# An attention and feed-forward block on one core: q's weights packed earlier, the second rows normalised in two parts, two value projections ahead of the scores, value slots by VectorE

## The chip, the core and the metric

The kernel runs on one core of a Trainium2 chip. A core has a matrix engine (TensorE, PE in the profile; its weight loads are shown apart as PEld), a vector engine (VectorE, DVE), a scalar engine for activations (ScalarE, ACT), a general engine (GpSimd, POOL) and a queue engine (SyncE, SP), and 16 DMA engines that move data. Each engine works through its own instructions in order. DMAs are issued by SP, ACT or POOL, and the issue itself takes time on that engine. The metric is the time of one execution on the device in microseconds, less is better; it is compared by the median of several runs.

## The reference

Four sequences of 1024 tokens with 256 channels go through an attention layer with 16 heads of 16 channels and then through a gated feed-forward part. Cut to what matters:

```python
x = x + _layernorm(attn(_layernorm(x), Wqkv, Wout))
x = x + _layernorm(ffn(_layernorm(x), w1, w2, h1, h2, w3))

# attn
qkv = (x @ Wqkv.T).reshape(B, S, 3, H, Dh)
scores = einsum('bhqd,bhkd->bhqk', q, k) / sqrt(Dh)
exp_x = exp(clip(scores - max(scores), -50, 50))
out = (exp_x / (sum(exp_x) + 1e-6)) @ v
return out @ Wout.T

# ffn
h = silu((x @ w1.T) * w1_s) * ((x @ w2.T) * w2_s)
h = gelu((h @ h1.T) * h1_s)
h = gelu((h @ h2.T) * h2_s)
return (h @ w3.T) * w3_s
```

## The kernel before

All tensors are in float32; products that need more than one pass are split into a high and a low part (`hi` and `lo`, type float32r). A batch is one of the four sequences; `h` counts its two halves of 512 rows (NH = 2), and a half has four row tiles of 128 (TPQ = 4).

**The opening (L1309 to L1341).** It prepares batch 0 before the loop over score tiles starts. Its parts are small steps, made by `prologue` (L329):

- `norm[h]`: statistics of the rows of a half on DVE (L97, L98), then the reciprocal root on POOL (L107).
- the first two steps of `xt[h]` (called `normalise[h]` at L1324): each applies mean and root to two of the four row tiles on DVE (L126, output `xn`).
- the last two steps of `xt[h]`: for each of two chunks of 128 channels, four transposes on PE (L363, into `pt`) and one copy of 128x512 into `xT`, which `to_scalar` (L324) does on ACT in the opening.
- `qk[0][h]`: two projections, of k (w = 1) and q (w = 0), 16 PE instructions each (L321). ACT then writes the high part (L324) and DVE the low part (L394). With the argument `(0, 1)` both chunks are done at once.
- `v`: four steps, each projecting the values of two row tiles (L321, into `pv`) and copying them to `cv`. In the opening the copy is ACT's, since `first_copy` looks at `alone` (L1314); after `alone = False` it is DVE's (L327).

`wqk_sb`, the weights of the projections, arrives padded to slots of 32 and is packed by `compact(w)` (L208), one ACT copy for k (w = 1) and one for q (w = 0).

**Stacks.** Scores are one product over a stack of 64 partitions, in which the high and low parts lie beside each other. `copies(g, w, c0, c1)` (L473) gives the 16 DMAs that fill the stack of one half of k or q for head group g; in the opening they are dealt over the queues in the order ACT, POOL, SP, POOL, SP, POOL, SP, POOL (L1319), so that each set of 16 takes two issues of ACT, eight of POOL and six of SP. Later stacks go by SP alone (L496).

**Value slots.** The weighing of values reads `vaug`, in which every head has 32 columns: 16 values and a one. `slots(b, g, t0, t1)` (L508) copies them there from `cv`, by POOL.

**The loop (L1357).** A tile is the scores of one block of 128 keys and two of the group's four heads with 512 queries: two products (L534, `s`), then one exponential on ACT (L535, `e`). A head group has 32 tiles, a batch four groups. Each turn of the loop makes up to three tiles, weighs earlier ones (L542, `acc`), folds maxima on DVE (L554, `top`), and then lets `side.take` run a few side steps: at most one with PE work in a turn. The side steps are chains, in the order in which they were added at L1344 to L1347: the rest of the values, the value slots, the projections for the upper channels (`qk[1]`), the next batch's preparation, stacks and later loads on SP, and the rounding of the feed-forward weights on POOL.

Buffers that matter: `pt`, the projections' outputs, `pv` in the opening and the scores share three PSUM buffers (`ps`); after the opening side steps use another single one (`misc`). `xn` has one buffer.

The order within an engine is the order of the program text: the scheduler of the language is off (L164).

Of the kernel before, what the change touches and what calls it, by code (L numbers as in the profile page):

```python
# [37 lines left out]
NQ = 512  # L38
# [91 lines left out]
def tile_fast(ctx: ExitStack, tc: tile.TileContext, x, wqk, wv, wo, w1, w1s, w2, w2s, h1, h1s, h2, h2s, w3, w3s, out, bad):  # L130
    nc = tc.nc
# [4 lines left out]
    NT = S // P  # L136
    NH = S // NQ
# [58 lines left out]
    with ExitStack() as actx, ExitStack() as rctx:  # L196
# [11 lines left out]
        def compact(w):  # L208
            nc.scalar.copy(wqk_sb[:, :, w], padded[:, :, w, :, 0:DH])  # L209
# [263 lines left out]
        def copies(g, w, c0=0, c1=S):  # L473

            m, i = g // GPT, g % 2

            def copy(u, j, n):
                def run(queue):
                    k = "hi" if (j // 2 == 0 if w == 0 else j % 2 == 0) else "lo"
                    r = (g % GPT) * HPG * DH + (2 * u + n) * DH  # L480
                    o = n * ROWS + j * DH
                    queue.dma_start(out=stacks[w, i, u][o : o + DH, c0:c1].bitcast(F32), in_=cq[w, m, k][r : r + DH, c0:c1].bitcast(F32))  # L482

                return run

            return [copy(u, j, n) for u in range(2) for j in range(PARTS) for n in range(2)]
# [18 lines left out]
            steps[0].ready = lambda: g < GPT or later["qk1"] == b  # L505
            return steps + [Step(done, 0, False)]

        def slots(b, g, t0=0, t1=NT):  # L508


            def run():
                nc.gpsimd.tensor_copy(  # L512
                    vaug[g % 2][:, t0:t1, :, 0:DH], cv[:, t0:t1, HPG * DH * g : HPG * DH * (g + 1)].rearrange("p t (h e) -> p t h e", e=DH)
                )
                slotted[g % 2] = b, g, t1

            return run
# [224 lines left out]
        side = Side()  # L742
        accs, tops, ends, later = {}, {}, {}, {"qk1": None}

        def add_flags(steps):

            if later.setdefault("flags", [[]])[0]:
                later["flags"][0].extend(steps)
            else:
                later["flags"] = side.add(steps)  # L750

        def begin(b):

            if b + 1 < B:
                norm, xt, qk, v, flags = prologue(b + 1, misc, to_vector)

                def first_made():
                    later["qk"] = b + 1
                    add_flags(flags[0])

                def second_made():
                    later["qk1"] = b + 1
                    add_flags(flags[1])


                steps = norm[0] + norm[1] + xt[0]
                for i, step in enumerate(qk[0][0]):
                    steps += [step, xt[1][i]]
                steps += xt[1][TPQ // 2 :] + qk[0][1]


                for m in range(DC):
                    qk[m][0][0].ready = lambda m=m: not any(at == b and g // GPT == m for at, g in outstanding)
                xt[0][TPQ // 2].ready = lambda: later["qk1"] == later["v"] == b
                v = v + [Step(lambda: later.update(v=b + 1), 0, False)]
                qk1 = sum(qk[1], [])
                for step in qk1:
                    step.gap = 2
                qk1 = qk1 + [Step(second_made, 0, False)]
                later["rest"] = [Step(lambda: side.add([Step(lambda: None, 5, False)] + qk1), 0, False)] + v  # L780

                later["chain"] = side.add([Step(lambda: None, 0 if b else 4, False)] + steps + [Step(first_made, 0, False)])

        def unit_end(b, g, h):
# [539 lines left out]
        normalise = [steps[: TPQ // 2] for steps in xt]  # L1324
        for step in norm[0] + normalise[0] + norm[1]:
            step.run()
        for h in range(NH):
            for step in xt[h][TPQ // 2 :]:
                step.run()
            for w, step in zip((1, 0), qk[0][h]):  # L1330
                if (h, w) == (0, 0):
                    compact(0)
                step.run(0, 1)
                for i, copy in enumerate(copies(0, w, h * NQ, (h + 1) * NQ)):
                    copy(queues[i % len(queues)])
                if w and h + 1 < NH:
                    for step in normalise[h + 1]:
                        step.run()
        stacked[0] = 0, 0
        v[0].run()  # L1340
        alone = False  # L1341
        load_x(1)
        early = [v[1], Step(slots(0, 0, 0, NT // 2), 0, False)]
        side.add(early + v[2:] + [Step(slots(0, 0), 0, False), Step(slots(0, 1), 0, False)] + sum(qk[1], []) + [Step(lambda: later.update(qk1=0, v=0), 0, False), Step(lambda: add_flags(flags[0] + flags[1]), 0, False)])  # L1344
# [12 lines left out]
        while weighed < len(tiles):  # L1357
# [14 lines left out]
            while halves and weighed + 2 <= n:  # L1372
                b, g, h, c, _ = tiles[weighed]
# [264 lines left out]
```

## Time and profile before

The median of three runs is 1232.06 us (1228.26 to 1233.94). The profiled execution took 1232.08 us, of which 1230.2 us lie between its first and last instruction.

| engine | busy us | share of the span | instructions |
|---|---|---|---|
| PE | 1169.1 | 95% | 7994 |
| PEld | 710.1 | 58% | 7994 |
| DVE | 841.5 | 68% | 1500 |
| ACT | 885.1 | 72% | 1049 |
| POOL | 209.1 | 17% | 279 |

The chain of work that ended last is made of PE for 58% of the span, of DVE and ACT for 12% each, of SP's queue for 6% and of DMA for 6%. Attention ends near 595 us; up to there the exponentials are busy for 483.1 us with 512 instructions of 1043 ns each, and the feed-forward part behind it is PE's, with four groups of 448 products of some 395 ns each.

In the rows shown below, a time is counted from the first instruction of the profile; a row stands for a run of like instructions, with its start, its busy time, engine, line, operation, output and inputs, and count. What stands in brackets is how long the engine was idle before it, and what ended that. "SPq" and "ACTq" are issues of DMAs on these engines. The granted clock is 1.00 at full speed.

### The profile page before, as it was taken

What the parts mean: (1) busy time and instruction counts of PE and PEld (TensorE: products, weight loads), DVE (VectorE), ACT (ScalarE), POOL (GpSimd) and SP (SyncE); (2) the same over time, 40 slices, a digit from 0 to 9 for tenths busy, and PEclk for the clock granted to TensorE, in tenths of its full rate; (3) what the DMA queues carried; (4) which work ended last, traced back from release to release, by engine and by line L of the source; (5) the groups of instructions that cost most, each with busy time, mean ns of one, the idle gap of its engine ahead of it and who ended that gap; (6) DMA issues with size and microseconds to landing.
All of it is one profiled execution on the core that took longest, in us unless ns stands there. A gap on an engine that the chain in (4) does not pass through costs nothing.

```text
span 1230.2 us, 21266 instructions
## 1 busy us (share of the span) xinstructions
PE 1169.1 (95%) x7994; PEld 710.1 (58%) x7994; DVE 841.5 (68%) x1500; ACT 885.1 (72%) x1049; POOL 209.1 (17%) x279
## 2 busy tenths in 40 slices
PE   7999999999999999999999999999999999999993
PEld 2333333333333333333578888887888878888783
DVE  3485668777687756868685756867578676784755
ACT  3798899878988989999457565576656766566651
POOL 6222035434354432000000000000000000000000
PEclk8999999999999999999999999999999999999997
DMA  4676755756666666453314341344512545125401
GB/s 132 175 183 152 172 148 134 186 135 175 152 162 154 173 168 148 96 140 128 104 34 138 119 156 52 103 171 147 178 59 97 175 156 176 62 82 199 155 7 37
DMA packets 78672, 163.66 MB, mean 133 GB/s; under 512 B 14688, under 2 KB 40928, under 8 KB 78560
## 3 DMA queue, kind: packets, MB, share of 16 engines
q1 hardware_dynamic: 68624, 131.27, 38.7%
q0 software_dynamic: 9408, 30.42, 7.7%
q8 instruction: 65, 1.06, 0.4%
q10 hardware_dynamic: 528, 0.52, 0.2%
q14 instruction: 47, 0.39, 0.1%
HBM read 98.71 MB, written 29.88 MB: 105 GB/s over the span
## 4 chain that ended last, share of the span: by engine, by line
PE 58%; DVE 12%; ACT 12%; SPq 6%; DMA 6%; issue 5%; ACTq 0%; POOL 0%; POOLq 0%; DVEq 0%
PE ph L1034 27%; PE acc L542 9%; PE pg L955 8%; ACT e L535 6%; PE s L534 6%; SPq L482 5%; PE p L321 3%; DVE lo L929 2%; ACT hi L925 2%; PE py L321 2%; DVE top L554 1%; DMA sq<-cq1lo 1%; DMA folded<-top_d 1%; PE pz L1139 1%; DVE w L1045 1%
## 5 line engine op out<-in xcount | busy, mean ns | idle before, releaser
L535 ACT ACTIVATE e<-s 128x1024 f32<-128x1024 f32 x512 | 483.1, 1043 | 53.8 <-PE s L534 44.1
L542 PE MATMUL acc<-e,vaug 128*32 128x512 f32 (+1 forms) x2424 | 258.7, 539 | 2.9 <-POOL vaug L512 2.9
L534 PE MATMUL s<-sq,sk 64*128 64x512 f32 x1024 | 189.3, 446 | 25.3 <-ACT e L535 17.1
L534 PEld LDWEIGHTS s<-sq,sk 64*128 64x128 f32 x1024 | 87.6, 185 | 172.0 <-ACT e L535 142.1
L1034 PE MATMUL ph<-hi,sq 128*128 128x512 f32 x448 | 178.1, 398 | 0.8 <-DVE w L1045 0.8
L1034 PE MATMUL ph<-lo,sq 128*128 128x512 f32 x448 | 176.7, 394 | 0.0
L1034 PE MATMUL ph<-hi,sk 128*128 128x512 f32 x448 | 176.7, 394 | 0.0
L1034 PE MATMUL ph<-lo,sk 128*128 128x512 f32 x448 | 176.4, 394 | 0.0
L107 POOL TENSOR_TENSOR rstd<-ve,minus_half 128x4 f32<-128x4 f32 (+1 forms) x34 | 38.2, 1123 | 740.6 <-DVE ve L105 681.8
L554 DVE TENSOR_TENSOR top<-top,e 128x512 f32<-128x512 f32 x192 | 138.9, 723 | 24.3 <-ACT e L535 18.5
L542 PEld LDWEIGHTS acc<-e,vaug 128*32 128x32 f32 x2424 | 61.8, 109 | 120.5 <-issue 107.8
L929 DVE TENSOR_TENSOR lo<-c,hi 128x1024 fp32r<-128x1024 f32 x48 | 58.4, 1223 | 66.0 <-ACT hi L925 66.0
L929 DVE TENSOR_TENSOR lo<-g,hi 128x1024 fp32r<-128x1024 f32 x48 | 58.8, 1226 | 58.0 <-ACT hi L925 57.7
L1034 PEld LDWEIGHTS ph<-hi,sq 128*128 128x128 f32 x448 | 84.2, 188 | 21.6 <-DVE w L1045 2.1
L1034 PEld LDWEIGHTS ph<-hi,sk 128*128 128x128 f32 x448 | 84.1, 188 | 20.0
L1034 PEld LDWEIGHTS ph<-lo,sk 128*128 128x128 f32 x448 | 84.1, 188 | 19.9
L1034 PEld LDWEIGHTS ph<-lo,sq 128*128 128x128 f32 x448 | 84.2, 188 | 19.1
L1022 ACT ACTIVATE c<-ph,h_scale 128x512 f32<-128x512 f32 x64 | 40.6, 685 | 50.1 <-PE ph L1034 50.1
L321 PE MATMUL p<-xT,wqk_sb 128*32 128x512 f32 x512 | 69.3, 622 | 4.7 <-ACT wqk_sb L209 2.6
L957 ACT ACTIVATE sg<-pg,w_scale 128x512 f32<-128x512 f32 x64 | 43.6, 688 | 35.7 <-PE pg L955 31.9
L1139 PE MATMUL pz<-w_sb,lo 128*128 128x256 f32 x256 | 61.6, 284 | 2.8 <-DVE lo L929 2.8
L958 DVE SCALAR_TENSOR_TENSOR g<-pg,w_scale,sg 128x512 f32<-128x512 f32 x64 | 47.7, 747 | 23.1 <-ACT sg L957 23.0
(183 smaller groups left out, 1735.1 us busy)
## 6 DMA issues: line engine op xcount, KB each, us to landing
sq<-h_f SPq DMA_DIRECT2D x56, 512.0 KB, 3.8
sk<-h_f SPq DMA_DIRECT2D x56, 512.0 KB, 4.5
w<-in_h_dram POOLq DMA_DIRECT2D x32, 256.0 KB, 5.2
h_f<-wr POOLq DMA_DIRECT2D x16, 512.0 KB, 4.3
x<-in_h_dram SPq DMA_DIRECT2D x16, 512.0 KB, 3.6
top_d<-top SPq DMA_DIRECT2D x30, 256.0 KB, 2.5
folded<-top_d SPq DMA_DIRECT2D x30, 256.0 KB, 3.2
h_f<-wr POOLq DMA_DIRECT2D x16, 384.0 KB, 3.7
```

What stands on the lines that cost most here:

```text
L321: nc.tensor.matmul(o[j : j + SLOT, :], w[:, j : j + SLOT], i, **flags)
L482: queue.dma_start(out=stacks[w, i, u][o : o + DH, c0:c1].bitcast(F32), in_=cq[w, m, k][r : r + DH, c0:c1].bitcast(F32))
L534: nc.tensor.matmul(s[:, a, :], stacks[1, g % 2, u][r, c * P : (c + 1) * P], stacks[0, g % 2, u][r, h * NQ : (h + 1) * NQ], start=True, sto ...
L535: nc.scalar.activation(pair(k)[:, u], s, AF.Exp)
L542: nc.tensor.matmul(acc[SLOT * i : SLOT * (i + 1), q0:q1], vaug[g % 2][:, c, i, :], pair(k)[:, i // 2, i % 2, q0:q1], start=c == 0 and q0 = ...
L554: nc.vector.tensor_max(top, top if c > 1 else pair(k - 2)[:, :, :, 0:P], pair(k)[:, :, :, 0:P])
L929: nc.vector.tensor_sub(self.lo[i].t, self.raw[i].t, self.hi[i].t.bitcast(F32))
L955: nc.tensor.matmul(p[:, k, :], homes[n][d][:, m * P : (m + 1) * P], half[:, d, :], start=d == j == 0, stop=d == DC - 1 and j == 1)
L957: nc.scalar.activation(sg, p[:, 0, :], AF.Silu, scale=scales["w1"][:, m : m + 1])
L958: nc.vector.scalar_tensor_tensor(x[i, h][c // 2].t[:, c % 2, :], p[:, 1, :], scales["w2"][:, m : m + 1], sg, ALU.mult, ALU.mult)
L1034: nc.tensor.matmul(p[:, j, :], w, half, start=start and c == n == 0, stop=c == HC // 2 - 1 and n == 1, skip_group_check=True,)
L1139: nc.tensor.matmul(p[:, j, :D], half[:, (t0 + j) * P : (t0 + j + 1) * P], homes["w3"][c], start=c == order[0] and n == 0, stop=c == order[ ...
```

## The change

It touches only the opening and the function `slots`.

- `compact(0)`, the packing of q's weights, is issued right after the turned first rows (`xT`) and ahead of k's high part; it was issued after k's stacks.
- The second rows' normalisation is issued in two parts of two row tiles: one ahead of k's low part, one behind it. Both stood behind it, together.
- k's DMA issues on ACT stay behind k's high part; q's two are held back until the second rows' `xT` copies have been issued.
- Two value projections run before the loop, not one; both are copied by ACT. The loop's first side step is now the third.
- The first half of group 0's value slots is copied before the loop and by DVE; the second half by DVE in the loop, where POOL copied the whole again. Group 1's slots stay with POOL.

```diff
-        def slots(b, g, t0=0, t1=NT):
+        def slots(b, g, t0=0, t1=NT, engine=nc.gpsimd):
 
 
             def run():
-                nc.gpsimd.tensor_copy(
+                engine.tensor_copy(
...
-        for h in range(NH):
+
+        def project_first(h, w):
+
+            qk[0][h][1 - w].run(0, 1)
+            runs = [(queues[i % len(queues)], copy) for i, copy in enumerate(copies(0, w, h * NQ, (h + 1) * NQ))]
+            for queue, copy in runs:
+                if queue is not nc.scalar:
+                    copy(queue)
+            return [copy for queue, copy in runs if queue is nc.scalar]
+
+        def turn_first(h):
+
             for step in xt[h][TPQ // 2 :]:
                 step.run()
-            for w, step in zip((1, 0), qk[0][h]):
-                if (h, w) == (0, 0):
-                    compact(0)
-                step.run(0, 1)
-                for i, copy in enumerate(copies(0, w, h * NQ, (h + 1) * NQ)):
-                    copy(queues[i % len(queues)])
-                if w and h + 1 < NH:
-                    for step in normalise[h + 1]:
-                        step.run()
+
+        turn_first(0)
+        compact(0)
+        normalise[1][0].run()
+        for copy in project_first(0, 1):
+            copy(nc.scalar)
+        normalise[1][1].run()
+        held = project_first(0, 0)
+        turn_first(1)
+        for copy in held:
+            copy(nc.scalar)
+        for w in (1, 0):
+            for copy in project_first(1, w):
+                copy(nc.scalar)
         stacked[0] = 0, 0
-        v[0].run()
+        for step in v[0:2]:
+            step.run()
+        slots(0, 0, 0, NT // 2, nc.vector)()
         alone = False
         load_x(1)
-        early = [v[1], Step(slots(0, 0, 0, NT // 2), 0, False)]
-        side.add(early + v[2:] + [Step(slots(0, 0), 0, False), Step(slots(0, 1), 0, False)] + sum(qk[1], []) + [...])
+        side.add(v[2:] + [Step(slots(0, 0, NT // 2, NT, nc.vector), 0, False), Step(slots(0, 1), 0, False)] + sum(qk[1], []) + [...])
         begin(0)
```

More of the change, by code (lines that the diff above doesn't have):

```diff
@@ L1326, in tile_fast @@
             step.run()
-        for h in range(NH):
+        def project_first(h, w):
[6 more added lines that the diff above has]
+        def turn_first(h):
             for step in xt[h][TPQ // 2 :]:
                 step.run()
-            for w, step in zip((1, 0), qk[0][h]):
-                if (h, w) == (0, 0):
-                    compact(0)
-                step.run(0, 1)
-                for i, copy in enumerate(copies(0, w, h * NQ, (h + 1) * NQ)):
-                    copy(queues[i % len(queues)])
-                if w and h + 1 < NH:
-                    for step in normalise[h + 1]:
-                        step.run()
+        turn_first(0)
[11 more added lines that the diff above has]
+                copy(nc.scalar)
         stacked[0] = 0, 0
-        v[0].run()
+        for step in v[0:2]:
+            step.run()
+        slots(0, 0, 0, NT // 2, nc.vector)()
         alone = False
         load_x(1)
-        early = [v[1], Step(slots(0, 0, 0, NT // 2), 0, False)]
-        side.add(early + v[2:] + [Step(slots(0, 0), 0, False), Step(slots(0, 1), 0, False)] + sum(qk[1], []) + [Step(lambda: later.update(qk1=0, v=0), 0, False), Step(lambda: add_flags(flags[0] + flags[1]), 0, False)])
+        side.add(v[2:] + [Step(slots(0, 0, NT // 2, NT, nc.vector), 0, False), Step(slots(0, 1), 0, False)] + sum(qk[1], []) + [Step(lambda: later.update(qk1=0, v=0), 0, False), Step(lambda: add_flags(flags[0] + flags[1]), 0, False)])
         begin(0)
```

## The prediction

> **What bounds the kernel now.** I read the page's 40 slices first, then the time-ordered rows of each engine over the first 75 us, because the diff touches only what is issued before the loop over score tiles and the first steps in it. The slices show TensorE (PE) at nine tenths or more everywhere but in the first and the last. So nothing of the later 1150 us is changed in its work; what can change is how long the opening takes, and whether the rest simply starts sooner. The rows of PE (start, duration, engine, line, operation, count, idle before and what ended it):
>
> ```profile
> 9.71 1.92 PE L321 MATMUL p<-xT,wqk_sb 128*32 128x512 f32 x16 [0.25 <-ACT xT L324]
> 14.27 3.62 PE L321 MATMUL p<-xT,wqk_sb 128*32 128x512 f32 x16 [2.64 <-ACT wqk_sb L209]
> 17.82 1.09 PE L363 MATMUL pt<-ident,xn 128*128 128x128 f32 x8
> 20.69 5.34 PE L321 MATMUL p<-xT,wqk_sb 128*32 128x512 f32 x32 [1.77 <-ACT xT L324]
> 25.84 1.91 PE L321 MATMUL pv<-wv_sb,xT 128*32 128x256 f32 x32
> ...
> 29.00 1.93 PE L321 MATMUL pv<-wv_sb,xT 128*32 128x256 f32 x32
> 30.87 0.97 PE L534 MATMUL s<-sq,sk 64*128 64x512 f32 x6
> 33.21 1.06 PE L542 MATMUL acc<-e,vaug 128*32 128x512 f32 x8 [1.37 <-POOL vaug L512]
> ...
> 42.51 1.50 PE L542 MATMUL acc<-e,vaug 128*32 128x256 f32 x16 [1.56 <-POOL vaug L512]
> ```
>
> Four holes are to be seen: 2.6 us before q's projection, 1.8 us before the second rows' projections, and twice a wait of the first weighings for POOL's copy into the value slots. The same 16 projection instructions take 1.92 us at 9.71 and 3.62 us at 14.27. The windows say why (busy time of PE, PEld, DVE, ACT, POOL with counts, then the granted clock, DMA share, GB/s); they are cut at the 3.41 us steps at which this trace's clock changes:
>
> ```profile
> 10.95:14.37 3.42, 0.78 (x12) 0.10 (x8) 2.05 (x6) 1.22 (x2) 2.76 (x4) 1.00 0.12 25
> 14.37:17.78 3.41, 3.41 (x16) 0.51 (x16) 0.00 (x0) 0.00 (x0) 2.47 (x6) 0.50 0.56 117
> 17.78:21.19 3.41, 1.64 (x20) 1.03 (x18) 0.69 (x1) 1.69 (x3) 2.35 (x5) 1.00 0.33 74
> 21.19:24.61 3.42, 3.42 (x24) 0.88 (x20) 0.01 (x1) 0.60 (x1) 1.48 (x4) 0.50 0.43 96
> ```
>
> A window in which PE was busy for 0.78 or 1.64 us is followed by one at half clock. ACT's rows show what filled the holes (ACTq is the issue of a DMA), and SP's what its queue does later:
>
> ```profile
> 12.33 1.23 ACTq L482 DMA_DIRECT2D sk<-ck0hi  x2
> 13.60 0.62 ACT L209 COPY wqk_sb<-e 128x512 f32<-128x512 f32 x1 [1.30 <-issue]
> ...
> 18.58 1.41 ACTq L482 DMA_DIRECT2D sq<-cq0hi  x2
> 20.04 1.09 ACT L324 ACTIVATE xT<-pt 128x512 f32<-128x512 f32 x2 [1.49 <-issue]
> ```
>
> ```profile
> 63.87 0.48 SPq L222 DMA_DIRECT2D wo_sb<-in_wo_dram  x1
> 69.47 0.38 SPq L572 DMA_DIRECT2D top_d<-top  x1
> ```
>
> **Part 1, q's weights packed early.** compact(0) goes from 13.60 to right behind the two xT copies, which end at 10.15, so it ends near 10.8. Its weights have landed: from 9.7 to 11.7 the DMA share is 0.00. ACT has nothing until 11.70, so the 0.62 us is hidden. q's projection then follows k's at 11.68 instead of 14.27 (2.59 us). The window 10.95:14.37 would then hold about 2.7 us of projections and some transposes, so no half clock should follow: 1.97 us instead of 3.66 (the chain's figures). q ends at 13.65, before 17.93. If the clock fell all the same, this gives back 1.7 us.
>
> Here the Trainium skill is weighed against the row. TensorE: Matmul & The Clock Gate (Part 1) gives half clock after an idle window of about 3.4 us, and its table of rules warns only of gaps over about 3 us. By it the holes of 2.6 and 1.8 us would leave the clock alone and only the holes could be won. The trace disagrees: over the grid of 3.41 us windows to 590 us, all five that were busy for 48% or less are followed by half clock, and none of those at 52% or more. I take the row; after the change no window of the opening should be under 70%. The skill's Part 4 speaks against me: transposes do not count as busy. Without them the hole is 13.65 to 15.2, at worst 1.6 of 3.41 us, still 54% busy, but near the edge; the grid of another execution may lie otherwise.
>
> **Part 2, the second rows in two parts.** POOL's root ends at 12.07. Two applies (1.38/4 = 0.345 us each) run to 12.8; k's low part (0.69) comes behind them, at 12.8 instead of 12.33; the other two end at 14.1. So the low part is 0.47 us later, and with it the first SP issue (13.05 to 13.5), which part 4 counts. The second transposes need the fourth row: last time the copy began 0.43 us after the fourth apply (8.63 to 9.06), so xT starts at 14.55, not 20.04. q's two DMA issues on ACT are now held until after the copies; that is the 1.41 us between cq0hi and xT. k's second projection starts at 14.55 + 0.61 + 0.04 = 15.2, not 20.69. It runs at full clock (1.97 for 3.25) to 17.2, q's to 19.1, v's first to 21.0. That step ended at 27.9: 6.9 us are won so far. The held issues, 15.7 to 17.1, fit before ACT's next work at 17.2.
>
> **Part 3, a second value projection ahead, slots by VectorE.** 1.91 us more before the first score: PE is free at 22.9. It only moves, since it stood at 29.00 between scores. Its copy out goes from DVE (0.69) to ACT (0.60), which idles then. The scores need q's stacked rows: SP's issue of those ends at 21.2 (part 4), plus 2.4 us to land, the median of sq: 23.6. The first tile uses the half that landed 2 us earlier. So two value projections and three tiles are done at about 24.7; before, they were done at 30.87: 6.2 us won.
>
> The DVE slots: no row of DVE copies 128x256 from SBUF; the nearest are the apply (0.345) and POOL's copy of that size (0.41). Between 0.2 and 0.5 I take 0.35, twice, on an engine that idles there (holes of 4.4 and 2.6 us before its rows at 36.07 and 39.36). They end near 24, before the weighing at 27. The second waits for v's last copy and holds up the next maxima by 0.35 at most. Both PE waits, 1.37 and 1.56, go: POOL had reached its copy at 32.75 only after sixteen stack issues, and its second at 41.51 rewrote all slots. From 30.87 to the fifth group's scores at 44.79 there were 13.92 us, of which 2.93 were these waits. Without them, but with one more half projection (0.86) because the side work is a step ahead, it ends at 24.7 + 11.85 = 36.5: **8.2 us**, with 0.86 us of work in hand. ACT agrees: its first exponential moves from 28.42 to 23.5, and of its 6.4 us of holes before 68 some 2.5 stay: 8.8.
>
> **Part 4, the queues.** The same 32 issues each: POOL's take 0.49 us, SP's stretches 3.95, 3.77, 4.16 and 3.70. Started at 13.5 and run through (a hole of 0.2 at 19.1 gone), SP ends its stacks at 29.0 instead of 33.27 and POOL near 28.7 instead of 32.75: SP is only 4.3 us ahead, less than PE. SP then works without a hole to 64.35: x, then the stacks of head group 1, whose last leaves at 61.21, now 56.9, and lands about 59.3. The tile that needs it was scored at 67.46, now 59.3: just in time, I charge 0.2. At 69.47 SP waited for the maxima after 5.1 us with nothing to do, so from there its queue follows the tiles again; it keeps pace if it is over 3.1 us ahead, and it is. The skill's SBUF — State Buffer (Who interferes with whom) says that a DVE operation in a 2-port mode blocks POOL's descriptor writing for its whole length; with six such operations near POOL's issues that is at most 6 x 0.35 = 2.1 us, POOL's end 30.8, still ahead. The row beside the applies now: POOL's issues took 0.70, 0.52 and 0.61 there, not 0.49: 0.36 in all. I take 0.3; nobody waits for it.
>
> **Sum.** 8.2 − 0.2 = 8.0 us. The profiled execution took 1232.08 us (span 1230.2 and 1.9 around it), and the median of the three is 1232.06, so I predict 1224.0. The later kernel repeats the same turns, each released by tiles; I charge it nothing.
>
> **Rivals.** (a) *SP sets the gain.* If its issues lengthen because they now meet in one block, or group 1 comes later than I count, PE waits at the first tile of group 1 and only SP's 4.3 us remain: 1227.8. For: SP has no hole from 25 to 64 us, and PE does wait 2.86 us for sq at 101.67. Against: the 5.1 us hole at 69. (b) *More.* The 0.86 in hand and a shorter wait at 101.67 (2.86) count fully: 8.0 + 0.9 + 1.9 = 10.8, 1221.3. (c) *Slower: the side steps, one turn earlier, meet the stack transfers.* Projections of the next batch overwrite cq while stacks are read from it; DVE already waits there in five places (14.0 us together, by the waits of DVE's low parts on sq and sk landings). A turn is 3.2 us; if each wait grows by a turn and stands on PE's path, 5 x 3.2 = 16 − 8 = 8 slower: 1240. It decides from 2.5 such turns on. Against: those steps are released only when their stacks have been issued. (d) *The clock drops once or twice anyway*: 1.7 to 3.4 us back, 1225.7 to 1227.4, joined with (a) in the range.
>
> **Numbers.** Forecast (1222.5 to 1225.5) 0.55; (a) and (d) 0.25; (b) 0.12; (c) 0.04; the gain lost in later turns, 1232, 0.04. A measurement here tells about 0.5%, 6.2 us, from no change, so under 1225.9 is faster: all of (b) and of the forecast and a little of (a), 0.68; slower 0.04; same 0.28. The range from 1219.5 to 1229.5 takes in (a), (b) and (d) with the medians' scatter.
>
> **What would show it.** Right: no half clock between 7.5 and 30 us; q's projection at 11.7 with 1.9 us; xT at 14.6; first exponential at 23 to 24.5; no PE wait on vaug; top_d of group 0 some 8 us before 69.47. Wrong: half clock at 14 or 21 us; PE waiting for sq near 59; new waits of DVE's low parts on transfers after 100 us.

## The result and the profile after

| | median us (range, runs) | ratio to before, 95% interval |
|---|---|---|
| before, in the same comparison | 1229.90 (1226.38 to 1233.94, 20) | |
| after | 1228.45 (1224.95 to 1232.57, 20) | 0.9990 [0.9978, 1.0002] |

No change can be told: the forecast of 1224.0 was 4.45 us too low, and its range, up to 1229.5, holds the time only because it reached to the rivals. About half of the miss is the starting point: the forecast began at 1232.06, a median of three, and twenty runs of before gave 1229.90. The profiled execution of after took 1230.18 us with a span of 1228.4, against 1232.08 and 1230.2.

The opening did what was forecast up to 22 us. PE's rows of after (start, duration, engine, line, operation, count, idle before and what ended it):

```profile
9.71 3.64 PE L321 MATMUL p<-xT,wqk_sb 128*32 128x512 f32 x32 [0.25 <-ACT xT L324]
...
15.16 3.64 PE L321 MATMUL p<-xT,wqk_sb 128*32 128x512 f32 x32 [0.25 <-ACT xT L324]
18.62 3.64 PE L321 MATMUL pv<-wv_sb,xT 128*32 128x256 f32 x64
22.91 0.70 PE L534 MATMUL s<-sq,sk 64*128 64x512 f32 x2 [0.66 <-DMA sq<-cq0hi]
25.02 1.07 PE L534 MATMUL s<-sq,sk 64*128 64x512 f32 x4 [1.41 <-ACT e L535]
26.02 3.47 PE L321 MATMUL pv<-wv_sb,xT 128*32 128x256 f32 x32
```

k's and q's projections are one run without a hole, the second rows start at 15.16 (20.69 before), and two value projections end at 22.3. Then PE waits twice, and the third value projection takes 3.47 us for what lasted 1.9. The windows of after (busy time of PE, PEld, DVE, ACT, POOL with counts; granted clock, DMA share, GB/s), cut at the 3.41 us steps at which this trace's clock changes, show why:

```profile
18.94:22.35 3.41, 3.32 (x64) 1.72 (x56) 0.69 (x1) 1.22 (x3) 3.08 (x8) 1.00 0.64 130
22.35:25.77 3.42, 1.45 (x6) 0.84 (x6) 0.37 (x1) 1.59 (x2) 3.42 (x8) 1.00 0.54 122
25.77:29.18 3.41, 3.41 (x34) 1.38 (x32) 0.00 (x0) 1.94 (x2) 3.15 (x7) 0.50 0.58 119
```

The two half-clock windows of before, at 14 and 21 us, are gone; a window with PE busy for 1.45 of 3.42 us is followed by a new one at 25.77. ACT's rows have the turned rows and the first exponential where they were expected (14.55; 23 to 24.5):

```profile
14.51 1.09 ACT L324 ACTIVATE xT<-pt 128x512 f32<-128x512 f32 x2 [0.31 <-PE pt L363]
...
23.65 1.02 ACT L535 ACTIVATE e<-s 128x1024 f32<-128x1024 f32 x1 [0.73 <-PE s L534]
```

SP's rows show the stack that PE waited for at 22.9 and, later, the maxima of group 0 (`top_d`, at 69.47 before). The second wait is for the same stack: its last transfer landed at 24.68, in the same moment in which the exponential ended that the bracket names.

```profile
17.34 2.03 SPq L482 DMA_DIRECT2D sq<-cq0hi  x1
...
51.70 0.53 SPq L572 DMA_DIRECT2D top_d<-top  x1
...
56.73 0.34 SPq L575 DMA_DIRECT2D folded<-top_d  x1
...
66.42 0.38 SPq L572 DMA_DIRECT2D top_d<-top  x1
```

One issue took 2.03 us where its neighbours take 0.5 to 0.8. And 66.42 instead of 69.47 is a gain of 3.05 us, not of 8.

**Where it went.** Exponentials are 512 in both kernels and in the same order, so their starts serve as a ruler. The lead of an exponential is its start in the profiled execution of before less its start in the run, in us (worked out from the rows of L535). The expectations further down count from another zero of the trace; their leads of after are 0.15 us higher.

```
exponential             0     12     33     45     48     64     80     96    112    256    511
after                4.77   4.92   4.78   4.67   2.93   2.93   2.79   3.04   0.89   1.75   2.10
e1_pack              5.00   3.60   3.60   3.59   3.59   3.59   4.66   4.65   2.68   3.49   4.13
e2_pool_slots        4.02   4.80   5.20   2.32   2.19   2.20   3.46   3.71   1.01   1.28   3.55
e3_three             2.93   6.21   5.91   3.11   2.98   2.98   1.96   2.20   2.66   2.16   4.73
e4_fill              4.49   6.52   4.92   4.41   3.92   3.92   2.34   2.57   2.95   2.64   3.46
f1_wo_pool           4.62   6.69   5.47   2.58   2.45   2.46   6.47   6.71   4.15   3.81   6.46
f2_wo_before         3.20   2.95   2.95   2.43   2.43   2.43   6.45   6.45   3.27   2.31   1.01
f3_back_late         4.63   5.06   5.49   5.10   5.10   5.09   5.82   6.17   3.06   8.36   8.92
f5_same_turn         5.06   4.91   4.89   4.89   4.89   4.89   5.96   6.20   6.22   7.06   9.66
g0_same_turn_timed   5.16   5.35   5.35   5.34   5.35   5.35   5.97   6.22   6.20   6.73   7.52
g1_turn_fill         4.94   6.71   6.71   6.70   6.70   6.71   6.66   6.91   4.75   5.27   6.03
g3_load_late         4.76   4.98   5.40   5.52   5.39   5.39   3.37   3.62   0.88  -1.22  -0.10
g4_lead_only         1.26   0.93   0.93   0.92   0.91   0.93   0.12   0.11   0.66   1.51   3.97
h1_turn_fill_pool    4.84   6.64   5.57   5.01   5.01   5.01   9.05   9.30   6.31   6.29   8.93
h2_same_turn_pool    4.50   3.82   3.80   3.29   3.29   3.30   7.33   7.57   3.24   3.91   4.53
```

Of the 8.2 us expected of the opening after has 4.92 at exponential 12; it loses 1.7 between 45 and 48, near 78 us, and 2.15 between 96 and 112, near 137 us. A row of this table is one execution, and the executions of one kernel scatter by 7.6 us in all (the range of after above). So the table is read for where a kernel loses, and the ratios for how much.

**The ruler itself lost its clock.** Before's own profile lies 2 us over its median, and its two half-clock windows at 14 and 21 us belong to that execution, not to the kernel. The run f2_wo_before (below) differs from before only behind 60 us. Its opening has the same two holes, and no half clock; q's projection takes 1.92 us, not 3.62, and it is 2.95 us ahead at exponential 12 with nothing changed there. Its rows and windows:

```profile
14.58 1.92 PE L321 MATMUL p<-xT,wqk_sb 128*32 128x512 f32 x16 [2.63 <-ACT wqk_sb L209]
19.05 3.64 PE L321 MATMUL p<-xT,wqk_sb 128*32 128x512 f32 x32 [1.52 <-ACT xT L324]
```

```profile
13.12:16.54 3.42, 1.96 (x17) 0.53 (x18) 1.54 (x5) 0.62 (x1) 3.39 (x7) 1.00 0.44 93
16.54:19.95 3.41, 1.89 (x19) 1.04 (x22) 0.69 (x1) 1.69 (x3) 3.08 (x8) 1.00 0.57 128
```

The steps of the clock lie elsewhere against the program here (the windows are cut at 3.41 us steps carried back from its first change, at 136.00), and split the holes, so that each window is busy for 55% or more. g4_lead_only, which keeps both holes too, shows the same. So some 3 us of every lead in the table are the bad luck of one execution.

The chain of waits of after over the second loss (start, duration, what):

```profile
51.70 4.95 DMA top_d<-top
...
56.73 3.76 DMA folded<-top_d
60.52 0.43 DVE folded L579
...
70.81 5.93 DMA folded<-top_d
76.76 0.44 DVE folded L579
...
77.85 0.59 DVE xT L327
78.48 1.06 PE p L321 x8
```

In before this chain runs over PE alone from 45 to 69.8 us:

```profile
44.86 0.90 PE s L534 x6
...
68.35 1.47 PE acc L542 x16
69.84 0.72 DVE o L787
```

In after it runs over SP's stacks, the maxima's way to memory and back, DVE's fold, which waits for it, and the copy of `xT` queued behind the fold, for which PE waits. The rows of DVE and PE, and of POOL, where 0.15 us ahead of that write stands the load of a feed-forward weight, 512 KB:

```profile
60.52 0.75 DVE L579 TENSOR_TENSOR folded<-folded 128x256 f32<-128x256 f32 x2 [1.83 <-DMA folded<-top_d]
...
76.76 0.75 DVE L579 TENSOR_TENSOR folded<-folded 128x256 f32<-128x256 f32 x2 [2.46 <-DMA folded<-top_d]
...
78.48 1.06 PE L321 MATMUL p<-xT,wqk_sb 128*32 128x512 f32 x8 [1.54 <-DVE xT L327]
```

```profile
51.55 0.61 POOL L270 DMA_DIRECT2D w<-in_w_dram  x1
```

The third loss is again a wait of PE, for a stack of q. PE's rows and two windows of after:

```profile
99.01 0.97 PE L534 MATMUL s<-sq,sk 64*128 64x512 f32 x2 [3.13 <-DMA sq<-cq1lo]
...
136.34 0.46 PE L534 MATMUL s<-sq,sk 64*128 64x512 f32 x1 [1.30 <-DMA sq<-cq1lo]
```

```profile
134.99:138.41 3.42, 1.94 (x14) 0.76 (x16) 1.95 (x4) 2.05 (x3) 0.00 (x0) 1.00 0.43 82
138.41:141.82 3.41, 3.41 (x36) 1.74 (x32) 0.00 (x0) 1.06 (x2) 0.00 (x0) 0.50 0.67 155
```

Before waited 0.76 us at that place and kept its clock; after waits 1.30 and has a half-clock window behind it. The wait near 99 was there before too. PE's rows of before:

```profile
101.67 0.95 PE L534 MATMUL s<-sq,sk 64*128 64x512 f32 x2 [2.86 <-DMA sq<-cq1lo]
...
138.85 0.46 PE L534 MATMUL s<-sq,sk 64*128 64x512 f32 x1 [0.76 <-DMA sq<-cq1lo]
```

**The clock and the scatter.** Each execution has a mean granted clock. Over the 125 executions of before that were timed beside the experiments, it goes with the time (correlation -0.86): twelve at 0.986 took 1233.0 us on average, eighteen at 0.990 took 1227.5. A half-clock window of 3.41 us lowers this mean by 0.0014. Before's mean is 0.9877 and that of after's twenty runs 0.9878. So on the whole the change has removed no half clock, where the forecast counted on two windows fewer, or 0.0028.

### The profile page after: what moved, and what is told of

The parts are those of the page before. It is cut to its first block, busy times and chain, and to the rows that moved or that the text cites. A ratio compares the mean times of both kernels' runs of the same rounds, so it can differ in the third digit from the quotient of the medians.

```text
span 1228.4 us, 21261 instructions
## 1 busy us (share of the span) xinstructions
PE 1168.8 (95%) x7994; PEld 710.7 (58%) x7994; DVE 838.8 (68%) x1501; ACT 885.6 (72%) x1050; POOL 207.9 (17%) x277
## 4 chain that ended last, share of the span: by engine, by line
PE 57%; ACT 14%; DVE 13%; issue 5%; SPq 5%; DMA 5%; POOL 0%; ACTq 0%; POOLq 0%; DVEq 0%
PE ph L1034 27%; PE acc L542 9%; ACT e L535 9%; PE pg L955 8%; PE s L534 6%; SPq L482 4%; DVE lo L929 2%; ACT hi L925 2%; DVE top L554 2%; PE p L321 2%; PE py L321 2%; PE pv L321 1%; PE pz L1139 1%; DVE w L1045 1%; ACT w L1022 1%
## 5 line engine op out<-in xcount | busy, mean ns | idle before, releaser
L535 ACT ACTIVATE e<-s 128x1024 f32<-128x1024 f32 x512 | 483.1, 1043 | 57.3 <-PE s L534 50.7
L321 PE MATMUL p<-xT,wqk_sb 128*32 128x512 f32 x512 | 65.7, 593 | 2.0 <-DVE xT L327 1.5
```

Source lines behind the costliest of these rows:

```text
L321: nc.tensor.matmul(o[j : j + SLOT, :], w[:, j : j + SLOT], i, **flags)
L535: nc.scalar.activation(pair(k)[:, u], s, AF.Exp)
```

## The experiments

Theory A: the lead is lost in separate events, each with a cause of its own (first stack and clock, the meeting near 51 to 78 us, the wait near 137). Theory B: SP's queue is the one limit, and caps any opening at some 3 us by exponential 64. Theory C, formed after the first four runs: the side steps now run one turn earlier against the tiles, since a value projection has left the loop, and so meet transfers that they did not meet.

**e1_pack**: before with the first edit alone.

```diff
             for w, step in zip((1, 0), qk[0][h]):
-                if (h, w) == (0, 0):
-                    compact(0)
...
+            if h == 0:
+                compact(0)
```

> The kernel before with q's weights packed early and nothing else. I measure the lead of exponential k: its start in the profile of before minus its start here. In the changed kernel the lead is 4.9 us at k = 0, 5.1 at k = 12, 3.1 at k = 64, 1.0 at k = 112 and 2.2 at k = 511. Theory A (the opening's gain is real and adds up, but was lost in three later places: PE idle until q's first stack has landed, with a half-clock window behind it; VectorE waiting for the folded maxima near 75 us; PE waiting for a stack near 136 us with a half clock behind it): q's projection at 11.7 for 1.9 us, k's second at about 16.4 instead of 15.2, first exponential near 24.5, lead at k = 12 about 4 because POOL's late slots stay. Theory B (SP's queue sets what is left after 60 us, whatever the opening does): the lead at k = 64 is again about 3 and the total 1 to 2 us below before. A by itself gives a total of about 1226.5 to 1229.

Measured: 1228.07 us (20 runs), ratio 0.9983 [0.9969, 0.9997]. By the medians this one line can't be told from the whole change. Its lead is flat at 3.6 from exponential 12 to 64, 0.65 more than f2_wo_before has with no edit there; its side steps stand in the turns of before, the maxima's write leaves at 50.64 and its read at 53.79, and no fold waits.

**e2_pool_slots**: after, with both copies of group 0's value slots on POOL as before.

```diff
-        slots(0, 0, 0, NT // 2, nc.vector)()
+        slots(0, 0, 0, NT // 2)()
...
-Step(slots(0, 0, NT // 2, NT, nc.vector), 0, False)
+Step(slots(0, 0), 0, False)
```

> The changed kernel with group 0's value slots copied by POOL, as before. POOL's stack issues end at 28.9, so the first weighing waits until about 29.4, which the changed kernel starts at 30.3 anyway: by theory A the first wait is nothing, the second (POOL copies all slots twice near 34) at most 1.5 us near 37, so the lead at k = 12 is 3.5 to 5. If VectorE's slots had been what cost time in the changed kernel (its copy before the maxima), the lead would be larger here. Theory B: lead at k = 64 near 3 in any case.

Measured: 1228.81 us in one run. PE's waits for POOL's slots are back, but as two of 0.65 and 0.66 us, not 1.37 and 1.56, which puts what DVE's slots save here at 1.3 us at most. The lead at 33, 5.20 for after's 4.78, says nothing against them: this execution kept its clock in the opening (third value projection in 1.93 us) where after lost it. Laid beside f1_wo_pool, which kept it too and has DVE's slots, it is 1.9 us behind at 12, of which 0.46 by a later first projection, and 0.3 at 33.

**e3_three**: after with three value projections ahead (`v[0:3]` leads, `v[3:]` remains).

> The changed kernel with three value projections ahead of the scores, not two. The third (1.9 us at full clock) lies where PE waited for q's first stack from 22.2 to 25.0, and its window is then busy, so theory A: no half clock at 25.7, this projection 1.9 us and not 3.5; first exponential later (24.6 instead of 23.5), but the lead at k = 3 about 3.5 instead of 1.6 and at k = 12 about 8 instead of 5.1. If A's losses downstream are separate events, the lead at k = 64 rises to about 5 and the total falls by 2 to 3 us against the changed kernel. Theory B: lead at k = 12 rises, but at k = 64 it is 3 again, and the total is that of the changed kernel.

Measured: 1228.85 us (20 runs), ratio 0.9985 [0.9970, 1.0000]. The third projection fills the wait for the stack: the first exponential comes later (lead 2.93), exponential 12 earlier (6.21 for 4.92). Nothing of it reaches the end.

**e4_fill**: after with idle products, whose result nobody reads, ahead of the first and second score tiles.

```diff
+        FILL = {0: 1, 1: 3}
+            for _ in range(FILL.get(k, 0)):
+                nc.tensor.matmul(filler[:, 0:D], ident, wv_sb[:, 0, :], start=True, stop=True)
```

> The changed kernel with four idle products into a spare buffer, one ahead of the first score tile and three ahead of the second, where PE waits for q's stack. No useful work is added or moved. Theory A says that half of the loss there is the clock: the window 22.2 to 25.7 is then more than half busy, no half clock follows, the third value projection takes 1.9 us instead of 3.5, and the lead at k = 3 rises from 1.6 to about 3, at k = 12 from 5.1 to about 6.6. If the clock is not the cause, nothing changes. Theory B: lead at k = 64 is 3.

Measured: 1229.50 us in one run. PE's rows of e4_fill, to be laid beside those of after from 22.91 on:

```profile
22.73 0.70 PE L1370 MATMUL filler<-wv_sb,ident 128*128 128x256 f32 x2
23.36 0.50 PE L534 MATMUL s<-sq,sk 64*128 64x512 f32 x2
23.79 1.56 PE L1370 MATMUL filler<-wv_sb,ident 128*128 128x256 f32 x6
25.28 0.73 PE L534 MATMUL s<-sq,sk 64*128 64x512 f32 x4
25.95 1.93 PE L321 MATMUL pv<-wv_sb,xT 128*32 128x256 f32 x32
```

The scores come no earlier, yet the projection takes 1.93 us instead of 3.47 and the lead at 12 is 6.52. So the half clock after the two waits costs some 1.5 us. That the idle products keep it away is likely, not certain: of the eight profiles with this opening and no such products six have the half clock, but e2_pool_slots and f1_wo_pool have not, with waits hardly shorter (0.33 and 1.17 us in f1, where a step of its clock, at 24.46, splits the second); of the three with them (e4, g1, h1) none has it. PE's rows of f1_wo_pool:

```profile
23.07 0.70 PE L534 MATMUL s<-sq,sk 64*128 64x512 f32 x2 [0.33 <-DMA sq<-cq0hi]
24.94 0.92 PE L534 MATMUL s<-sq,sk 64*128 64x512 f32 x4 [1.17 <-ACT e L535]
25.79 1.93 PE L321 MATMUL pv<-wv_sb,xT 128*32 128x256 f32 x32
```

By exponential 64 e4_fill has lost 2.6 of its lead again: its fold waits 3.75 us.

**f1_wo_pool** and **f2_wo_before**: after, and before, with the 16 loads of `wo` issued by POOL instead of SP.

```diff
-                    rest.append(load(wo_sb[DH * h : DH * (h + 1), c, :], wo[r : r + DH, :]))
+                    rest.append(load(wo_sb[DH * h : DH * (h + 1), c, :], wo[r : r + DH, :], nc.gpsimd))
```

> The changed kernel with the sixteen loads of the output weights (wo) issued by POOL instead of SP, some 8 us of SP's issue time between 63 and 107 us. The first four runs left 2.3 to 3.9 us of lead at k = 64 whatever the lead at k = 12 had been (3.2 to 6.5), which speaks for theory B. If SP's queue is the limit there, PE's wait of 3.1 us for sq at 99 goes, and with it the half clock behind it: the lead at k = 80 rises from 2.9 to about 7, and the total falls by 3 to 5 us against the changed kernel. If the lead was lost to other things (the fold on VectorE near 76 us alone, theory A's separate events), the lead at k = 80 changes by less than 1.5 us.

> The kernel before with the same sixteen loads on POOL. It also waits for sq at 101.7 (2.9 us) with a half clock behind it. If SP is the limit for both, this one gains up to 4.5 us at k = 80 too, about 1226 to 1228 in all, and what is between it and the changed kernel with the same edit is the opening's gain as it would be without that limit: 4 to 5 us. If the limit is not SP: under 1.5 us against before.

Measured: f1 1224.49 us (11 runs), ratio 0.9952 [0.9935, 0.9968]; f2 1226.95 (20 runs), 0.9973 [0.9960, 0.9985]. In both the lead rises by 4.0 us between 64 and 80, since the wait near 99 has gone. The two are the fair pair for the opening, since neither has a half-clock window there: at exponential 12 they are 3.7 us apart, at 64 not at all, and 2.5 us by the medians, where 4 to 5 was expected. PE's later rows of f1_wo_pool:

```profile
96.61 0.68 PE L534 MATMUL s<-sq,sk 64*128 64x512 f32 x2 [0.24 <-ACT e L535]
...
133.39 1.73 PE L534 MATMUL s<-sq,sk 64*128 64x512 f32 x4 [2.01 <-DMA sq<-cq1lo]
```

At 133 the wait is longer than in after (2.01 for 1.30), and 2.6 us are lost there. That f1 keeps its interval clear of after's is a thing shown: SP's queue did cost at 99. That f1 has lost 2.9 us between 33 and 45, as theory B and A both allow, says nothing between them.

**f3_back_late**: after with the reading back of the maxima one turn later, for the first batch (`Step(back, 3, ...)` for `Step(back, 2, ...)`).

> The changed kernel with the read back of the folded maxima one turn later in the first batch, so that SP does not stand at 54.7 waiting for their write to land, and VectorE reads them a turn later. Theory A: the waits of VectorE for the folded maxima at 60 (1.8 us) and 76 (2.5 us) go, PE's wait for xT at 78 (1.5 us) goes, the lead at k = 48 and 64 is 4.8 instead of 3.1, and this stays to the end (total 1.7 us less). Theory B: the lead at k = 64 rises, but PE's wait for sq near 99 grows by the same amount, so that at k = 80 it is 3 again.

Measured: 1223.12 us in one run. The lead stays at 5.1 from 45 to 64, and the first fold, now at 62.56, doesn't wait: with read and fold one turn later, the way of the maxima to memory and back is covered again. The second, at 76.94, still waits 1.41 us, but PE doesn't wait for what stands behind it. Between 112 and 256 this execution gains 5.3 us where after gains 0.9, so its time is no measure of the edit.

**f5_same_turn** and **g0_same_turn_timed**, one kernel: after with an empty step that takes one turn ahead of the side steps, so that PE's order is that of before from the second turn on.

```diff
-        side.add(v[2:] + ...
+        side.add([Step(lambda: None, 1, False)] + v[2:] + ...
```

> The changed kernel with an empty first side step in the place of the value projection that was moved out, so that every later side step stands in the same turn as before, and PE's order is the same as before from the second turn on. If it is the side steps' earlier turn that costs (rival c of the prediction: POOL's weight load at 51.6 beside the write of the maxima at 51.7, the fold on VectorE before its data), the fold's waits go and the lead at k = 48 is that at k = 12, about 5 to 6; if SP's queue is the limit, the lead still falls to about 3 by k = 80, with a longer wait for sq near 97.

> The kernel of f5_same_turn again, timed. Its one look gave 1222.4 us and a lead that stayed at 4.75 from k = 12 to k = 64 and grew afterwards, so theory B (SP's queue as the limit) falls, and theory C takes its place: what cost the changed kernel its lead is that every later side step of VectorE, POOL and PE came one turn earlier while SP's did not. C expects a median of 1221 to 1224.5, clear of the changed kernel's 1228.5; if the one look was a lucky execution, the median is above 1226.

Measured: 1222.41 us in the first run, 1226.62 (22 runs), ratio 0.9975 [0.9963, 0.9987], when timed: the single run was one from the low end of the scatter, and theory C's sum is missed. The lead is flat from 12 to 64 in both executions, as C expects, and the chain of g0_same_turn_timed has PE and exponentials alone where that of after had DMA and DVE:

```profile
51.62 0.86 PE p L321 x8
52.47 0.90 PE s L534 x6
53.37 1.43 PE acc L542 x16
```

Part of the missing sum is the clock: the mean of the 22 runs is 0.9864, that of after's 0.9878, about one half-clock window lower. The empty step leaves PE less to do in the opening, and all three profiles with it and without idle products (f5, g0, h2) have half clock there, for 3.4 or 6.8 us.

**g1_turn_fill**: the idle products of e4_fill and the empty step of f5_same_turn together.

> f5_same_turn with the idle products of e4_fill, that is, side steps in the same turn and no half clock while q's stack lands. By C and the clock's share of the opening (e4_fill: lead at k = 12 of 6.5 instead of 5.1) the lead at k = 12 is 6 to 7 and stays there to k = 64; the total is 1 to 2 us below f5_same_turn, 1220 to 1223. If a greater lead meets SP's queue after all, the lead falls again between k = 33 and 80 and the total is that of f5_same_turn.

Measured: 1226.14 us (13 runs), ratio 0.9959 [0.9943, 0.9974], clear of after's interval. The lead is 6.7 at 12 and still 6.7 at 64; then PE waits 3.05 us near 95, and at 132.5 it has waited 1.35, drops its clock and loses 2.2. The mean clock is 0.9888, 0.0024 over that of g0_same_turn_timed (standard error 0.0007).

**g3_load_late**: after, with POOL's second weight load alone one turn later (an empty step of one turn between the first and second `round_weights`); all that is behind it on POOL moves with it, nothing on the other engines.

> The changed kernel with POOL's second load of weights (and all behind it on POOL) one turn later; PE's, VectorE's, ACT's and SP's order is untouched. In the changed kernel that load (512 KB) was issued at 51.6, beside the write of the maxima at 51.7, which then took 5 us to land while SP stood; in f5_same_turn and e1_pack it came 2 to 3 us after the write, which landed in 3.2. If the collision is what made the read back late, SP's read back is issued near 55 instead of 56.7, VectorE's fold waits at 60 and 76 shrink by more than half, and the lead at k = 64 is 4 to 5. If it is rather the turn in which VectorE folds, the waits and the lead of 3.1 at k = 64 stay.

Measured: 1232.33 us in one run. The load left at 59.47 instead of 51.55, the write of the maxima at 49.95, its read at 53.11, and no fold waited; the lead is 5.39 at 64 where after has 2.93. So the second loss goes with this edit, but in this one execution SP also reached the write 1.75 us earlier than in after, which alone would nearly cover the fold's wait of 1.83. The time shows the next loss: PE waits 3.77 us for `sq<-cq1lo` near 97 and has 6.8 us of half clock behind it, and from there this execution lies where before does.

**g4_lead_only**: before with only the second value projection ahead of the loop (`v[1].run()` behind `v[0].run()`), so that the side steps run one turn earlier but the opening isn't shortened otherwise.

> The kernel before with nothing but the second value projection moved ahead of the scores, so that its side steps stand one turn earlier as in the changed kernel, without the packing, the two-part normalisation or VectorE's slots. Theory C: the lead is about -1.5 at k = 0 and 0 to 1.5 at k = 12; the fold on VectorE waits for its data near 65 and 80, and the total is 0 to 3 us slower than before. Against C: the lead at k = 64 and at the end is that at k = 12.

Measured: 1228.44 us in one run. The weight load left 4.55 us after the write of the maxima (51.86), and the lead is 0.9 from 12 to 64. So in this execution the earlier turn alone costs nothing up to there: theory C, taken as "one turn earlier is late", falls, and "one turn earlier, with the transfers meeting" remains.

Over fifteen profiles (f3_back_late, whose read is moved on purpose, is left out): where the weight load left within 0.5 us of the maxima's write (after, e2, e3, g1, h1) the read left 5.03, 5.02, 5.32, 3.15 and 5.05 us after the write; in the ten others, with the load 1.8 us or more away, it was 3.02 to 3.51. So the meeting is likely to make the write slow, though not in every execution, g1 being the exception. What parts g1 from the other four is the order: in those the load left 0.48 us ahead of the write to 0.01 behind it, and the write took 4.94 to 5.24 us to land; in g1, and in f3_back_late, the load left 0.14 and 0.23 us behind it, and the write took 2.78 and 2.60. That the order decides was not tried. In e4 and f1 the fold waited without a slow write: SP reached the write at 53.08 and 52.96 only, behind two stack issues that took 4.86 and 4.57 us. What is common to all folds that waited is that the fold stood before its data in DVE's order, for either reason.

**h1_turn_fill_pool** and **h2_same_turn_pool**: g1 and f5 with the `wo` loads on POOL as in f1. What was still open was whether the turn and SP's queue are two losses that add up, or one.

> The kernel g1_turn_fill (side steps in the turns of before, idle products in the opening's gaps) with the 16 loads of wo issued by POOL instead of SP. The turns take the lost lead away at 45 to 80 (lead 6.7 at k=64, time 1226.1), the wo loads at 80 to 112. If the two losses are separate and add up: wait for sq<-cq1lo at 95 under 0.8 us (3.05 in g1_turn_fill), lead at k=80 9 to 11, at k=112 7 or more, median 1221 to 1224. If one limit stands behind both (the chain of SP's transfers, or the later tiles): lead at k=112 no more than 5, median 1224.5 to 1226.5 as f1_wo_pool and g1_turn_fill alone.

> The kernel f5_same_turn (side steps in the turns of before, no idle products) with the 16 loads of wo issued by POOL. If the losses add: lead at k=64 4.7 to 5.4, at k=80 8.5 to 9.5, no wait over 0.8 us near 95, median 1222 to 1225. If not: lead at k=80 6 to 6.5 and median 1224.5 to 1226.6. If h1_turn_fill_pool beats it by more than 1 us, the idle products of the opening carry through to the end; so far (g1_turn_fill 1226.1, g0_same_turn_timed 1226.6) they do not.

Measured: h1 1222.42 us (9 runs), ratio 0.9932 [0.9908, 0.9957]; h2 1225.57 (14 runs), 0.9955 [0.9939, 0.9970]; before beside them 1230.54 (22 runs). PE's rows of h1_turn_fill_pool:

```profile
94.05 0.67 PE L534 MATMUL s<-sq,sk 64*128 64x512 f32 x2 [0.25 <-ACT e L535]
...
131.34 1.72 PE L534 MATMUL s<-sq,sk 64*128 64x512 f32 x4 [2.55 <-DMA sq<-cq1lo]
```

The wait near 95 has gone and the lead rises by 4.03 us between 64 and 80 in both, as it did in f1 and f2. So up to exponential 96 the two losses are separate, whatever the lead was. In the times they add up with the idle products only: h1 is the fastest version here, faster than both kernels of the change, but h2, with turns and `wo` loads alone, is no faster than f1 with the loads alone (1225.57 and 1224.49), and its lead at 80, 7.33, lies between the two expectations. h1's leads reach the low end of what was expected at 80 (9.05 for 9 to 11) and miss it at 112 (6.31 for 7): in this execution the load met the write again (0.48 us apart, 1.6 us lost between 12 and 45), and at 131 PE waited 2.55 us and lost its clock. The idle products do carry through here. The runs of h1 and h2 were timed together: h1's mean is 2.6 us lower (standard error 0.9), and its clock 0.9909 for 0.9872 (standard error 0.0008), which is some 2.6 half-clock windows fewer, an estimate by the 0.0014 above.

## Why the prediction was wrong

**Parts 1 and 2, wrong in a term of 3 us.** "1.97 us instead of 3.66" for q's projection and "1.97 for 3.25" for k's second took the half clock of one execution for the kernel's. f2_wo_before has the old opening without it, 2.95 us earlier at exponential 12, and the mean clock of after's runs is that of before's. The text saw that "the grid of another execution may lie otherwise", but asked this of the new opening only, not of the old one. Between the two openings at full clock (f1, f2) lie 3.7 us, not 8.2.

**Part 1, else right.** q's projection follows k's as forecast. No half clock at 14 and 21 us in any profile with this edit.

**Part 2, else right.** `xT` at 14.51 for 14.55, the second projections at 15.16 for 15.2. POOL's end of part 4, 28.9, was 28.7 in the text.

**Part 3, right in what it removes, wrong in two terms.** The waits for POOL's slots are gone, DVE's copies took 0.37 and 0.29 us (0.35), the first exponential began at 23.65. But SP's issue of q's stack, which "ends at 21.2 (part 4), plus 2.4 us to land", failed: one issue took 2.03 us, SP ended this stack at 22.85, and three tiles were done at 26.1 instead of 24.7: 1.4 us. An issue of 1.4 to 2.1 us stands at this place in all twelve profiles with this opening, so it belongs to the change; its cause is open. And "no window of the opening should be under 70%" failed with it: 1.45 of 3.42 us is 42%, and the half clock after it took 1.5 us more, as e4_fill shows. The rule weighed there (the Trainium skill, TensorE: Matmul & The Clock Gate, table of "Why this matters for your kernels": beware of gaps over about 3 us) would have passed these waits of 0.66 and 1.41 us too; this trace again disagrees, that of f1_wo_pool agrees. 8.2 − 1.4 − 1.5 = 5.3, and 4.92 was measured on the same ruler. The term left out is the window between the last value projection and the second tile: the text made sure of the windows with projections, and moved a projection away from where it covered the stack's landing.

**Part 4, wrong.** "SP then works without a hole to 64.35" and "it keeps pace": SP stood still from 54.73 to 56.73, because its read of the maxima waits for their write, and everything behind it in SP's order stood too. The long issue had made SP end the opening's stacks at 30.46, not 29.0; with the standstill it ended group 1's at 60.77, not 56.9. The wait for them at the first tiles of group 1 was small all the same: 0.19 us at 62.68, for the 0.2 that was charged. The loss came through DVE: fold, then `xT`, then PE.

**The sum, wrong.** "The later kernel repeats the same turns, each released by tiles; I charge it nothing" is the step that cost most of what the opening did gain: 1.7 us near 78 and 2.15 near 137. A wait of 0.76 us at 138.85 in before was not weighed; it was 0.4 us short of the shortest that lost the clock there. Of the rivals (a) with 1227.8 came closest in size, by luck, since its wait at group 1 took 0.19 us; (d) was right that a half-clock window comes, and (c) in place: the earlier side steps did meet transfers, but at one point and for 1.7 us, not at five for 16. The entry nearest to what happened, "the gain lost in later turns", had a chance of 0.04.

**The theories.** A holds for the places: the losses sit apart, and e4, f5 and f1 each take one away without the others. In the times only the `wo` loads are clear by themselves (f1, f2). B falls: leads of 4.9 to 6.7 at exponential 64 with SP's queue unchanged (f5, g0, g1, g3). It is right about the wait near 99 alone. Of C the stage is shown, the sum is not: the turn brings 1.8 us by medians (g0's interval overlaps after's), and nothing beside the `wo` loads (h2 and f1). Why the wait near 131 to 138 is 0.3 us in some of these kernels and 2.5 in others was not tried.

## What to carry to other kernels

When an opening gets shorter, the gain lasts only as long as each later place has slack for it: follow the earlier work to the first queue that takes things in order, and look at what stands behind its waiting entries. A part that is moved ahead of a loop leaves a turn of the loop, and all side steps move up against the tiles and the transfers; keeping their turns with an empty step is one edit. Before a hole is left in the matrix engine while a transfer lands, put work into it: the hole costs its length and, in some executions, the clock behind it. And before a half-clock window of one profile is counted as a gain, look whether other executions of the same kernel have it.

## What the runs showed of the hardware

- **The clock changes on a grid of 3.41 us that doesn't start with the program.** Every half-clock stretch of the attention part in the sixteen profiles is 3.41 or 6.83 us long. The grid lies elsewhere in each execution: a step falls at 14.34 us in before, at 13.12 and 16.54 in f2_wo_before. The same holes of 2.6 and 1.5 to 1.8 us took the clock twice in the one and not at all in the other.
- **Short waits can take the clock.** At the wait near 131 to 138, the clock was halved for 3.4 us or more in every profile with 1.1 us of waiting or more (ten, from 1.12 to 2.55) and in none with 0.82 or less (six). By busy share the line isn't sharp: windows with PE busy for up to 62% (132.95 in e1_pack) were followed by half clock, others with as little as 48% (575.55 in f3_back_late) were not. So the limit of 48 to 52% in the prediction doesn't hold; what else decides is open.
- **Single DMA issues stretch.** One took 2.03 us on SP where 0.5 to 0.8 is usual; in e4_fill two (`sk<-ck0lo` at 36.88) took 4.86 for 1.22. Everything behind them on SP came later.
- **One kernel's executions differ by more than the change.** The same kernel gave 1222.4 in one run and a median of 1226.6 in 22; its leads at 511 in two profiles were 9.7 and 7.5. Much of it is the clock: 0.001 of mean granted clock goes with 1.2 us (a straight line through the 125 runs of before).
